# Block products for the gates of four more tiles in the first pass of a float32 macaron layer, later weight loads, and two reordered steps of the attention and drain stages

## The chip, the cores and the metric

The kernel runs on one core of one Trainium2 chip. The metric is device microseconds (us) of one execution. A core has five engines with a queue of instructions each: TensorE (PE in the profile; its weight loads are PEld), VectorE (DVE), ScalarE (ACT), GpSimd (POOL) and SyncE (SP, which here only issues DMAs). Each queue runs in order, and an instruction may wait for semaphores that other engines or DMAs raise.

## What is computed

The reference, cut to what matters (x is 4 x 1024 x 1024 in float32, so 4096 tokens of 1024 channels; the FFN weight is 1024 x 1024; there are 64 centroids):

```python
def _L0_ffn_ref(input, weight, bias, centroids, assignments):
    dots = softmax(x @ centroids.T / 0.1)          # gates: one row of 64 for each token
    hits = dots > 0.01
    query_sel = any(hits, axis=1)                  # which tokens are kept
    row_sel = any(hits, axis=0)[assignments]       # which output columns are kept
    dense = x @ weight.T + bias
    return where(query_sel[:, None] & row_sel[None, :], dense, 0)

x = x + 0.5 * _L0_ffn_ref(_layernorm(x), ...)
x = x + _L0_attn_ref(_layernorm(x), ...)           # attention among the 32 heads of one token
x = x + 0.5 * _L0_ffn_ref(_layernorm(x), ...)
```

`row_sel` needs the gates of all tokens before any column can be kept or dropped. So each FFN is a pass over all tokens for its products and gates, and the masked addition comes in the pass behind it.

## The kernel before

The 4096 tokens are 32 tiles of 128. There are three passes over them: the first FFN's products and gates (lines 511 to 791), the attention with the first FFN's masked addition ahead of it and the second FFN's gates behind it (lines 794 to 1174), and the second FFN's products and final addition (lines 1177 to 1263). Weights stay in SBUF: `wc` holds the 1024 columns of the FFN weight (transposed) with the 64 centroid columns behind them, `wqkv` holds the 768 columns of query, key and value (the four query heads of a group summed to one).

**Products of two tiles at once.** `winograd` (L293) computes columns 0 to 767 of two tiles a and b (a pair) with seven half products in place of eight: sums of the two tiles' activations (`token_sums`, L271, four POOL subtractions or additions: s1 to s4, of 128x512 each, in two "row" tiles named ts) meet sums of weight blocks (`weight_sums`, L262: ts, in the tiles ws). It is a generator with a `yield` behind each product, so that the loop around it sets where each product stands. Its order is product 1 (into a PSUM bank u), 5 (into v), 2, then 6 added onto u, 7 (into y), 3, then 4 added onto y. DVE adds each bank to the result row at L306; product 6 can only start once DVE has read u, and 4 once it has read y. `last_two` (L372) does the same for the 320 columns behind column 767, of which the last 64 are the gates: seven products of 160 columns each (L389, tiles la) with weight sums of their own (`te`, two of which lie in buffers that are used for something else later: `mask` and `bqkv`). Where a tile does not use it, `ffn_part` (L244) computes the 320 columns with eight plain products (L241, tiles ff).

**First pass.** Tiles 0 to 3 and 28 to 31 get their gates from `logits` (L684: ff products, then `gate` at L430 on DVE: maximum and subtraction). For tiles in `GATED`, here 8 to 27, `last_two` runs in step with `winograd` (L730 to 733). Tiles 4 to 7 are not in it and use `logits` too. The loop over t (L708) issues for each t, in this order: loads of later tiles on SP, stores of finished pairs on SP, normalization of tile t+1 on ACT (L535), moments of tile t+4 on DVE (L170), `logits` of tile t if it is not in GATED, the first product of the current pair, the block transpose of tile t+1 on DVE (L235), the scales of tile t+4, the exponentials of gates on ACT (L443), the other products (four in all at odd t, three at even t), `gated` (L446, four DVE operations for each tile that end with an update of `best`, L455), one step of `esums` (the sums te, one POOL subtraction each) at t = 5 to 8, token sums at odd t, and last a step of `weights(t)` (L601): one load of Wq (SP, 512 KB) with a reduction on DVE one iteration later (L612) at t = 3 to 5 and 11 to 15, and loads of Wk and Wv with copies on POOL (L627) at t = 16 to 19. The pair a = t - 3 and a + 1 is in work at odd t and at t + 1.

**Attention pass.** The loop over s (L1018) works on the projections of tile s, the attention of tile b = s - 2, the output of tile g = s - 3 and the gates of tile f = s - 4 or a = s - 5. From s = 4 projections are done by pairs (`project_two`, L813, the same seven products; its product 5 needs s1 of the pair's token sums, tiles ts_2q). At odd s the POOL queue holds, in order: `keys` (L888), `second_added` (L975, L979: the attention's result onto x), a store of x (L1051), `store_2` of two tiles (L996, L997: four DMA issues), `first_added` of tile s + 3 (L504: the first FFN's masked rows onto x; the mask itself is applied on DVE at L493), and then the four token sums of the pair that starts at s + 1 (L1095). At the next s, ACT reads that tile s + 3 at L196.

**Drain of the attention pass.** From s = 32 no new tile starts, and pairs of the second FFN's products (`winograd` on banks of the shared pool, weight sums in `wqkv`) fill PE. `gates_used` (L1007) runs `gated` for each tile whose gates are done. At s = 34 (NT + 2) it stands at the head of the step (L1052), ahead of three products of the pair 28, 29 (L1102); behind them on DVE come the moments of tile 31 (L170), then the adds of u and v (L306) behind product 6. On PE, product 6 is followed by the transpose of tile 30 (L218) and the ff products of tile 29 (L241), whose PSUM bank is the one that v had.

Of the kernel before, what the change touches and what calls it, by code (L numbers as in the profile page):

```python
# [32 lines left out]
PARTS = ((0, HALF), (HALF, 2 * HALF), (2 * HALF, EMB + NCL))  # L33
KEPT = 6
LAST = 2 * HALF, (EMB + NCL) // 2 - HALF
GATED = range(8, 28)
PAIRED = range(4, 32)
WARM = 16
ROWS = 26
# [3 lines left out]
def kernel(  # L43
# [42 lines left out]
    NT = xf.shape[0] // P  # L86
# [60 lines left out]
    def row(name):  # L147
        return data.tile([P, EMB], F32, tag="row", bufs=ROWS, name=name)
# [62 lines left out]
    def transposed(xn, name):  # L211

        t_ = row(f"xT_{name}").rearrange("p (k c) -> p k c", c=P)
        for h in range(2):
            tp = bank(f"tp_{name}_{h}").rearrange("p (j c) -> p j c", j=4)
            for j in range(4):
                k = 4 * h + j
                nc.tensor.transpose(tp[:, j, :], channels(xn)[:, k], ident)  # L218
            nc.scalar.copy(t_[:, 4 * h : 4 * h + 4, :], tp)  # L219
        return t_  # L220
# [225 lines left out]
    def gated(es, t, which):  # L446

        e, sm = es
        nc.vector.reciprocal(sm, sm)
        top = small.tile([P, 1], F32, tag="gtop", name=f"gtop_{which}_{t}")  # L450
        nc.vector.tensor_reduce(top, e, AX.X, ALU.max)
        nc.vector.tensor_scalar(
            qsel[which][:, t : t + 1], top, sm, THRESHOLD, ALU.mult, ALU.is_gt
        )
        nc.vector.scalar_tensor_tensor(best[which], e, sm, best[which], ALU.mult, ALU.max)  # L455
# [55 lines left out]
    with (  # L511
# [89 lines left out]
        def weights(t):  # L601


            if 3 <= t < 6 or 11 <= t < 16:

                k = t - 3 if t < 6 else t - 8
                qn = row(f"qn{k}").rearrange("p (c r) -> p c r", r=REP)
                nc.sync.dma_start(
                    out=qn.rearrange("p c r -> p (c r)"), in_=channel_rows(wq)[k]
                )  # L610
                yield
                nc.vector.tensor_reduce(  # L612
                    by_head(wqkv[:, k, :], 0),
                    qn.rearrange("p (d g) r -> p d g r", g=HKV),
                    AX.X,
                    ALU.add,
                )
            elif 16 <= t < 20:
                k = 2 * (t - 16)
                kvs = row(f"kv{k}").rearrange("p (k w c) -> p k w c", k=2, w=2)  # L620
                for i, src in ((0, wk), (1, wv)):
                    for j in range(2):
                        nc.sync.dma_start(out=kvs[:, j, i], in_=channel_rows(src)[k + j])
                yield
                for j in range(2):
                    for i in range(2):
                        nc.gpsimd.tensor_copy(  # L627
                            by_head(wqkv[:, k + j, :], i + 1),
                            kvs[:, j, i].rearrange("p (d h) -> p d h", h=HKV),
                        )  # L630
            elif 20 <= t < 24:

                nc.sync.dma_start(out=wtd[t - 20], in_=blocks(wc)[t - 20])
            elif t == 25:
                next(qsums)
            elif t == NT - 4:
                asg = load_assigned()
                yield
                hot.append(one_hot(asg))
            elif t == NT - 3:  # L640
                bn = row("bn_q").rearrange("p (c r) -> p c r", r=REP)
                nc.sync.dma_start(
                    out=bn.rearrange("p c r -> p (c r)"),
                    in_=bq.rearrange("d h -> (d h)").partition_broadcast(P),
                )
                bss = row("bs")
                bs = {i: bss[:, (i - 1) * D * HKV : i * D * HKV] for i in (1, 2)}
                for i, src in ((1, bk), (2, bv)):
                    nc.sync.dma_start(
                        out=bs[i], in_=src.rearrange("d h -> (d h)").partition_broadcast(P)  # L650
                    )
                yield
                nc.vector.tensor_reduce(
                    by_head(bqkv, 0), bn.rearrange("p (d g) r -> p d g r", g=HKV), AX.X, ALU.add
                )
                for i in bs:
                    nc.gpsimd.tensor_copy(
                        by_head(bqkv, i), bs[i].rearrange("p (d h) -> p d h", h=HKV)
                    )

        pending = iter(())
        sc, sb, ss, es, ge = {}, {}, {}, {}, {}
# [45 lines left out]
        for t in range(3, NT):  # L708

            loads(t)  # L710
            for i in (5, 6) if t == 3 else (t + 3,):
                if i in sc:
                    sb[i] = spread(sc.pop(i), i)
            if t % 2 == 1 and t > 4:
                for i in (a, a + 1):
                    nc.sync.dma_start(out=d1[i], in_=dt_.pop(i))
            ahead_b = t + 1 in sb and t > 3
            if ahead_b:
                blocks_normed(t + 1, sb.pop(t + 1))
            if t + 4 < NT:  # L720
                mv = moments(xt.pop(t + 4), f"1_{t + 4}")
            if t not in GATED:
                es[t] = logits(t)
            if t == 3:
                xT[4] = transposed(xn.pop(4), "1_4")
            if t % 2 == 1:
                a = t - 3
                s4 = ss.pop(a)
                steps = winograd(a, a + 1, s4, ts, psum1, 1, held=t == NT - 1)
                if a in GATED:  # L730
                    for i in (a, a + 1):
                        dt_[i] = row(f"d1_{i}")
                    steps = zip(steps, last_two(a, a + 1, s4, te, ge))
            if t < NT - 1:
                next(steps)
            if ahead_b:
                xT[t + 1] = from_blocks(t + 1, 1)
            if t + 4 < NT:
                block_scales(t + 4, mv)
            for i in sorted(es):  # L740
                if i >= t - 3 and not isinstance(es[i], tuple):
                    es[i] = gate_exp(es[i], i, 0)
            if t == NT - 1:
                for i in sorted(es):
                    gated(es.pop(i), i, 0)
                break
            for _ in range(2 + t % 2):
                next(steps)
            for i in (t - 3, t) if t < 6 else sorted(es):
                gated(es.pop(i), i, 0)  # L750
            if t % 2 == 0:
                for i in sorted(ge):
                    es[i] = gate_exp(ge.pop(i), i, 0)
            if 5 <= t < 9:
                next(esums)
            if t % 2 == 1:
                ss[t - 1] = token_sums(xT, t - 1, t, 1)
            for _ in pending:
                pass
            pending = weights(t)  # L760
            next(pending, None)

        xn2, xT2 = {}, {}
# [28 lines left out]
    with (  # L794
# [190 lines left out]
        es = {}  # L985

        def has(t):
            return 0 <= t < NT
# [18 lines left out]
        def gates_used():  # L1007
            for a in sorted(es):
                gated(es.pop(a), a, 1)
                if a < FIRST_KEPT:  # L1010
                    store_2(a)
# [6 lines left out]
        for s in range(NT + 5):  # L1018
            b, g, f, a = s - 2, s - 3, s - 4, s - 5
            paired, odd = s in PAIRED, s % 2 == 1  # L1020
# [28 lines left out]
                next(sums)  # L1049
            if g >= 0 and g < FIRST_KEPT:  # L1050
                nc.gpsimd.dma_start(out=y2[g], in_=xt[g])  # L1051
            if (odd or not paired) and s not in (NT, NT + 1):  # L1052
                gates_used()
            if s == 4:
                next(qsums)
# [30 lines left out]
            if paired and odd:  # L1086
                gate_2(a)
                qkv[s] = rearranged(flat.pop(s), s)
                fo = attend(st, qkv.pop(b)[1], b)
                if s + 2 in xn2:  # L1090
                    xT2[s + 2] = transposed(xn2.pop(s + 2), f"2_{s + 2}")
                if s + 3 in dt_ and has(s + 3):
                    first_added(s + 3)
                if s + 1 in PAIRED:
                    ss2 = token_sums(xT2, s + 1, s + 2, "2q")  # L1095
            if paired and not odd:
                fo = attend(st, qkv.pop(b)[1], b)
                if has(s + 2):
# [1 line left out]
            if s == NT + 2:  # L1100
                dt_[a] = row(f"d3_{a}")
                steps = winograd(s - 6, s - 5, ss, ts, None, 3)  # L1102
                for _ in range(3):
                    next(steps)
            for _ in range({NT: 3, NT + 1: 2}.get(s, 0)):
                next(steps)
            if NT <= s < NT + 2:
# [19 lines left out]
            else:  # L1127
                between()
                k = s - NT
# [15 lines left out]
            if odd and not paired and s + 1 in PAIRED:  # L1145
                xT2[s + 2] = transposed(xn2.pop(s + 2), f"2_{s + 2}")
                ss2 = token_sums(xT2, s + 1, s + 2, "2q")
            if 1 <= s <= 3:
# [3 lines left out]
                i = {1: NT - 4, 3: NT - 2}.get(s)  # L1152
# [24 lines left out]
    with (  # L1177
# [30 lines left out]
        t = NT - 2  # L1208
# [98 lines left out]
```

## Time and profile before

| | us |
|---|---|
| three runs | 1303.0 median (1300.79 to 1303.44) |
| profiled execution | 1301.45 |
| its span, first to last instruction | 1299.7 |
| mean granted TensorE clock in it | 0.998 |
| first pass, PE's first ff to the end of the pairs before 404 us | 14 to 404 |
| attention pass with its start and drain | 404 to 1040 |
| third pass | 1040 to 1300 |
| busy: PE, PEld, DVE, ACT, POOL | 1286.0, 833.2, 889.2, 490.4, 641.1 |

All rows below come from the profiled execution. Times in them count from the start of its span; a line such as L306 is a line of the kernel before. In a row of the timeline, the columns are start, duration, engine, line, operation, names of output and inputs, shape, count, and in brackets the engine's idle time ahead of it and what ended it. One matmul of the program shows as two records in float32, so eight plain products of a tile are 16 records, and one half product (four matmuls) is eight. Records of PE overlap, because matmuls are pipelined: what a group costs PE is the time from its start to the start of the next, not its duration.

### The profile page before, as it was taken

The page shows a single profiled execution, that of the slowest core. Times are in us where ns is not written, and L with a number is a line of the kernel's source. Part 1 is how long each engine was busy: PE and PEld are TensorE (multiplying, and loading weights), DVE is VectorE, ACT ScalarE, POOL GpSimd, SP SyncE. Part 2 cuts the span into 40 slices and gives each one's busy share as a digit, 9 for nine tenths or more (in the row PEclk, how much of TensorE's full clock was granted, in tenths as well). Part 3 has the DMA queues.
Part 4 walks back from the last instruction along what each step waited for, and adds up shares of the span by engine and source line. Part 5 has one row for each costly group of instructions (what it writes and reads, how often), then busy time and mean ns, then how long its engine had stood idle before and what let it go on. Part 6 is the DMA issues. An engine that isn't in the chain of part 4 may idle for free.

```text
span 1299.7 us, 22528 instructions
## 1 busy us (share of the span) xinstructions
PE 1286.0 (99%) x8634; PEld 833.2 (64%) x8634; DVE 889.2 (68%) x1810; ACT 490.4 (38%) x792; POOL 641.1 (49%) x512
## 2 busy tenths in 40 slices
PE   8999999999999999999999999999999999999998
PEld 7665677777776666666666666666666655555555
DVE  4566667665646358888888888888877449555556
ACT  4443332333210446666676676666633300000000
POOL 2631212312113256777877777776857417533440
PEclk9999999999999999999999999999999999999999
DMA  8645645654114156577777777777552347665522
GB/s 302 143 150 150 177 158 150 182 195 137 60 57 194 44 168 199 175 219 222 226 216 232 236 223 223 225 235 214 173 161 61 106 158 222 235 211 181 175 111 85
DMA packets 191124, 227.08 MB, mean 175 GB/s; under 512 B 118184, under 2 KB 146728, under 8 KB 191016
## 3 DMA queue, kind: packets, MB, share of 16 engines
q1 hardware_dynamic: 170892, 171.33, 44.4%
q0 software_dynamic: 11232, 37.49, 8.3%
q10 hardware_dynamic: 8892, 16.81, 3.6%
q8 instruction: 68, 1.11, 0.4%
q14 instruction: 40, 0.33, 0.1%
HBM read 134.59 MB, written 90.99 MB: 174 GB/s over the span
## 4 chain that ended last, share of the span: by engine, by line
PE 87%; DVE 5%; POOL 3%; ACT 2%; DMA 2%; issue 2%; SPq 0%; ACTq 0%; POOLq 0%
PE st L315 43%; PE qs L832 16%; PE ff L241 11%; PE la L389 6%; PE pq L241 3%; PE tp L218 3%; PE po L950 2%; PE sc L908 2%; DVE o L962 1%; DVE bn L170 1%; DMA qk<-qkvd 1%; PE tpw L584 1%; POOL wqkv L268 1%; DMA cn<-in_L_ffn_centroids_dram 0%; DVE d L493 0%
## 5 line engine op out<-in xcount | busy, mean ns | idle before, releaser
L280 POOL TENSOR_TENSOR ts<-xT 128x512 f32<-128x512 f32 x32 | 41.9, 1309 | 358.9 <-DVE sc L179 159.0
L241 PE MATMUL ff<-wc,xT 128*128 128x320 f32 x704 | 197.1, 433 | 1.3 <-ACT xT L219 0.6
L306 DVE TENSOR_TENSOR d<-st,d 128x384 f32<-128x384 f32 (+1 forms) x162 | 88.7, 549 | 155.7 <-PE st L315 154.5
L315 PE MATMUL st<-wc,xT 128*128 128x384 f32 x512 | 175.8, 486 | 0.0
L241 PEld LDWEIGHTS ff<-wc,xT 128*128 128x128 f32 x704 | 131.9, 190 | 56.2 <-ACT xT L219 1.5
L315 PEld LDWEIGHTS st<-wc,xT 128*128 128x128 f32 x512 | 95.9, 190 | 61.8 <-issue 0.6
L315 PE MATMUL st<-wqkv,ts 128*128 128x384 f32 (+1 forms) x392 | 129.7, 480 | 2.1 <-DVE d L306 1.9
L315 PE MATMUL st<-ws,ts 128*128 128x384 f32 x384 | 131.1, 486 | 0.0
L832 PE MATMUL qs<-wc,ts_2q 128*128 128x384 f32 x336 | 114.6, 491 | 1.8 <-POOL ts_2q L280 1.8
L315 PEld LDWEIGHTS st<-wqkv,ts 128*128 128x128 f32 x392 | 73.8, 190 | 52.9 <-POOL x L979 2.4
L306 DVE TENSOR_TENSOR d<-st,brow 128x384 f32<-128x384 f32 x96 | 52.8, 550 | 74.4 <-PE st L315 74.3
L888 POOL TENSOR_TENSOR kd<-qk,tmask 128x1024 f32<-128x1024 f32 x32 | 62.6, 1955 | 82.6 <-DMA qk<-qkvd 82.4
L173 ACT ACTIVATE mv<-mv,eps 128x1 f32<-128x1 f32 x66 | 19.5, 295 | 216.8 <-DVE mv L172 216.5
L504 POOL TENSOR_TENSOR x<-x,d 128x1024 f32<-128x1024 f32 x32 | 75.7, 2366 | 48.3 <-DVE d L493 44.6
L315 PEld LDWEIGHTS st<-ws,ts 128*128 128x128 f32 x384 | 71.2, 190 | 43.0 <-issue 0.8
L832 PEld LDWEIGHTS qs<-wc,ts_2q 128*128 128x128 f32 x336 | 62.5, 190 | 46.0 <-POOL ts_2q L280 3.0
L493 DVE SCALAR_TENSOR_TENSOR d<-d,qsel,mask 128x1024 f32<-128x1024 f32 (+2 forms) x68 | 88.4, 1299 | 0.2
L315 PE MATMUL st<-wc,ts 128*128 128x384 f32 x256 | 87.9, 486 | 0.0
L170 DVE BATCH_NORM_STATS2 bn<-x 128x6 f32<-128x512 f32 x132 | 84.2, 679 | 3.0 <-DMA x<-in_L_attn_x_dram 3.0
L979 POOL TENSOR_TENSOR x<-x,ot 128x1024 f32<-128x1024 f32 x32 | 80.3, 2509 | 2.5
L219 ACT COPY xT<-tp 128x512 f32<-128x512 f32 x112 | 59.5, 582 | 52.6 <-PE tp L218 52.6
L832 PE MATMUL qs<-wqkv,xT 128*128 128x384 f32 x224 | 78.3, 492 | 0.0
(147 smaller groups left out, 2309.3 us busy)
## 6 DMA issues: line engine op xcount, KB each, us to landing
x<-in_L_attn_x_dram SPq DMA_DIRECT2D x64, 512.0 KB
d<-d SPq DMA_DIRECT2D x64, 512.0 KB
out_dram<-x ACTq DMA_DIRECT2D x30, 512.0 KB
xb<-in_L_attn_x_dram SPq DMA_DIRECT2D x108, 128.0 KB
y<-x POOLq DMA_DIRECT2D x26, 512.0 KB, 4.1
xTd<-xT POOLq DMA_DIRECT2D x26, 512.0 KB, 6.1
xT<-xTd SPq DMA_DIRECT2D x26, 512.0 KB
x<-y SPq DMA_DIRECT2D x26, 512.0 KB
```

What stands on the lines that cost most here:

```text
L170: nc.vector.bn_stats(st[:, i, :], src[:, i * 512 : (i + 1) * 512])
L219: nc.scalar.copy(t_[:, 4 * h : 4 * h + 4, :], tp)
L241: nc.tensor.matmul(p, src[:, k, :], wts[:, k, lo:hi], start=(k == 0), stop=(k == KT - 1))
L280: nc.gpsimd.tensor_tensor(s1, a21, a22, ALU.add)
L306: nc.vector.tensor_tensor(out, ps, other, ALU.add)
L315: nc.tensor.matmul(ps, src[:, k, :], wts[:, k, :], start=(k == 0 and onto is None), stop=(k == 3), skip_group_check=onto is not None,)
L389: nc.tensor.matmul(ps, src[:, k, :], wts[:, k, :], start=(k == 0 and onto is None), stop=(k == 3), skip_group_check=onto is not None,)
L493: nc.vector.scalar_tensor_tensor(d[:, sl], d[:, sl], qsel[which][:, t : t + 1], mask[:, sl], ALU.mult, ALU.mult)
L504: nc.gpsimd.tensor_tensor(xt[t], xt[t], dt_.pop(t), ALU.add)
L832: nc.tensor.matmul(ps, src[:, k, :], wts[:, k, :], start=(k == 0 and onto is None), stop=(k == 3), skip_group_check=onto is not None,)
L888: nc.gpsimd.tensor_tensor(kd, qk[:, :, D:].unsqueeze(2).to_broadcast([P, NBLK, 4, D]), tmask.unsqueeze(1).unsqueeze(3).to_broadcast([P, NB ...
L979: nc.gpsimd.tensor_tensor(xv, xv, ov, ALU.add)
```

## The change

It has three parts. In the first pass, `GATED` begins at tile 4: the pairs 4, 5 and 6, 7 run `last_two`, and the `logits` of those four tiles go. For that, the four `esums` steps stand at t = 3 to 6, the eight loads of Wq with their reductions at t = 7 to 14 and the loads of Wk and Wv at t = 15 to 18. In the attention pass at odd s, s1 and s2 of the token sums stand ahead of `first_added` on POOL, and s3 and s4 behind it. In the drain at s = 34, `gates_used` stands behind the three products of the pair 28, 29 in place of ahead of them.

```diff
-GATED = range(8, 28)
+GATED = range(4, 28)
...
         def weights(t):
-            if 3 <= t < 6 or 11 <= t < 16:
-                k = t - 3 if t < 6 else t - 8
+            if 7 <= t < 15:
+                k = t - 7
...
-            elif 16 <= t < 20:
-                k = 2 * (t - 16)
+            elif 15 <= t < 19:
+                k = 2 * (t - 15)
...
             for i in (t - 3, t) if t < 6 else sorted(es):
-                gated(es.pop(i), i, 0)
+                if i in es:
+                    gated(es.pop(i), i, 0)
...
-            if 5 <= t < 9:
+            if 3 <= t < 7:
                 next(esums)
...
-            if (odd or not paired) and s not in (NT, NT + 1):
+            if (odd or not paired) and not NT <= s <= NT + 2:
                 gates_used()
...
+                more = []
+                if s + 1 in PAIRED:
+                    ss2 = token_sums(xT2, s + 1, s + 2, "2q", more)
                 if s + 3 in dt_ and has(s + 3):
                     first_added(s + 3)
-                if s + 1 in PAIRED:
-                    ss2 = token_sums(xT2, s + 1, s + 2, "2q")
+                for i in more:
+                    i()
...
                 steps = winograd(s - 6, s - 5, ss, ts, None, 3)
                 for _ in range(3):
                     next(steps)
+                gates_used()
```

With a list as its last argument, `token_sums` issues s1 and s2 and appends a function that issues s3 and s4.

## Prediction

> **What bounds the kernel now.** I read the page first, then PE's waits, then the timelines of the three places that the change touches.
>
> ```profile
> span 1299.7 us, 22528 instructions
> PE 1286.0 (99%) x8634; PEld 833.2 (64%) x8634; DVE 889.2 (68%) x1810; ACT 490.4 (38%) x792; POOL 641.1 (49%) x512
> PE st L315 <- DVE d L306: 1.9, 1, 1.9
> PE qs L832 <- POOL ts_2q L280: 1.8, 2, 1.4
> PE ff L241 <- DVE d L306: 0.4, 1, 0.4
> ```
>
> The first two lines are of the page, the others of PE's waits (who, for whom, us in total, times, longest). PE is at work for 99% of the span, so time goes only where PE issues less or waits less. Every other engine has a third of the span free: what the change moves there is free until it makes PE wait. Three of the listed waits lie where the change works, 4.1 us together; the rest (tile loads at the start and the like) it does not touch.
>
> A busy PE need not be at its pace, so I took the distances from start to start. In the first pass they repeat to the nanosecond:
>
> ```profile
> 90.81 4.47 PE L241 MATMUL ff<-wc,xT 128*128 128x320 f32 x16
> 95.11 2.74 PE L315 MATMUL st<-wc,xT 128*128 128x384 f32 x8
> ...
> 133.81 1.25 PE L389 MATMUL la<-wc,xT 128*128 128x160 f32 x8
> 134.90 2.74 PE L315 MATMUL st<-ws,ts 128*128 128x384 f32 x8
> 137.48 1.25 PE L389 MATMUL la<-te,ts 128*128 128x160 f32 x8
> ```
>
> A plain gate product costs 95.11 - 90.81 = 4.30 (4.31 at the others), a narrow block product 134.90 - 133.81 = 1.09, a wide one 137.48 - 134.90 = 2.58.
>
> **Part 1, gates of tiles 4 to 7.** Removed: four ff products, 4 x 4.31 = 17.2. Added: two pairs of seven la products, 14 x 1.09 = 15.2. PE gains 2.0. A check by stages: pair 2, 3 with its two ff takes 68.60 to 95.28, 26.68; pair 8, 9 takes 131.23 to 156.90, 25.67; the difference is 1.01 for each pair.
>
> The narrow products are not new to the trace: it has 70 of them, all at this pace, against the same weights. A row that could speak against them is PEld's 190 ns for each load: 112 loads in a row would be 21.3, 4.1 more than the ff products took. But eight la records start within 1.09, 136 ns each, so most of each load is under the matmul before it. The Trainium skill, "TensorE: Matmul & The Clock Gate", section "LDWEIGHTS (loading the stationary operand)", gives a load by its columns over 1.2, which would be an estimate of 107 ns here, below 136; by that page too nothing is added. I take 0.
>
> What moves. PE reaches pair 4, 5 earlier by three ff products (those of tiles 4, 5 and 6), at about 82 in place of 95. What must be there by then:
> - te: POOL needs 1.55 for each. One comes ahead of the sums of pair 2, 3 (43.6 to 45.2), two behind them (50.2 to 53.3), the last behind the sums of pair 4, 5 (about 66). Their first uses are from 82 on. The sums of pair 2, 3 end 1.6 later, at 50.2, and PE needs them at 62.6.
> - Tiles 5 to 7 are not needed by PE at their own t any more, but with their pairs. DVE transposed tile 5 at 59.65 to 61.67, tile 7 at 86.3 to 88.3; with PE ahead these come earlier still, for their inputs (ACT at 48.75 for tile 5) were there.
> - SP loses three loads of 512 KB in its busiest stretch (46.9, 53.1, 67.8) and gets them at t = 7 to 10 instead, where one for each t stands beside the same stores and loads as at t = 11 to 15 now; PE has no wait there. DVE's reductions (1.2 each) go with them.
> - PE passes tiles 4 to 6 at 7.7, 10.3, 7.7 each. It does so now at t = 8 to 10 (105 to 131) without a wait.
>
> One place is tight, at t = 4. DVE does the gates of tiles 0 and 3 (53.82 to 55.08) and the moments of tile 8 (to 56.6) ahead of the add of product 7, which would end at 57.15. Product 4 writes the same bank and can start at 52.25 + 2 x 2.58 = 57.41. Margin 0.26. The `best` operations in that stretch took 0.28 each while POOL was idle; where POOL ran, at 65.24 and 66.10, they took 0.50 and 0.87. Stretched like the longer, two would add 1.2 and PE would wait 0.9. POOL now works there until 53.3, while the first `best` comes at 54.25: clear by 0.95. Bounds 0 to 0.9; I take 0. The Trainium skill, "SBUF — State Buffer", section "Who interferes with whom", makes this an exclusive lock between DVE and GpSimd for an instruction with two SBUF inputs, so that a `best` which meets POOL waits it out, up to 1.55; by that rule the cost is all or nothing, and the 0.95 decides it.
>
> **Part 2, token sums ahead of the addition.** Product 5 of a pair waits for s1, which stands on POOL behind `first_added`:
>
> ```profile
> 908.12 2.36 POOL L504 TENSOR_TENSOR x<-x,d 128x1024 f32<-128x1024 f32 x1
> 910.43 1.26 POOL L280 TENSOR_TENSOR ts_2q<-xT 128x512 f32<-128x512 f32 x1
> 911.75 2.52 PE L832 MATMUL qs<-wc,ts_2q 128*128 128x384 f32 x7 [1.36 <-POOL ts_2q L280]
> ```
>
> Without L504 ahead of it s1 ends 2.3 earlier. Its input, the transposed tile, left ACT at 902.97, so nothing else holds it. The waits of 1.36 and of 0.40 (at 602.82) go: 1.7 by start to start. In the other pairs s1 ended 0.5 to 1.4 ahead of product 5 (636.12 against 637.07), so nothing is gained there; a margin of about 3 replaces it. s3 and s4 end as before.
>
> The price is that x of tile s + 3 is ready 2.5 later, when s2 ended until now. Its reader is ACT's L196 at the next s. In an ordinary pair: x would end at 637.5, L196 starts at 639.12, margin 1.6. In the pair above: 913.0 against 912.29, so ACT is late by 0.7; DVE asks for the outcome at 918.47 (L202), and ACT's last step for it ended at 916.3. Hidden. Bounds: 0 to a delay on twelve steps (rival 4). I take 0. `keys`, which stands behind s4, keeps its time.
>
> **Part 3, gates of tile 28 behind three products.**
>
> ```profile
> 1012.37 0.16 DVE L449 RECIPROCAL gsm<-gsm 128x1 f32<-128x1 f32 x1 [3.03 <-ACT ge L443]
> ...
> 1012.81 1.46 DVE L455 SCALAR_TENSOR_TENSOR best<-ge,gsm,best 128x64 f32<-128x64 f32 x1
> 1014.20 0.54 DVE L306 TENSOR_TENSOR d<-st,brow 128x384 f32<-128x384 f32 x1
> 1014.84 0.56 DVE L306 TENSOR_TENSOR d<-st,d 128x384 f32<-128x384 f32 x1
> ...
> 1014.88 2.82 PE L315 MATMUL st<-wqkv,ts 128*128 128x384 f32 x8 [1.86 <-DVE d L306]
> ...
> 1018.94 1.34 PE L241 MATMUL ff<-wc,xT 128*128 128x320 f32 x4 [0.35 <-DVE d L306]
> ```
>
> DVE stood for 3 us on ACT's exponential with the add of u queued behind it, and product 6 waited for that add. With the add first it runs at 1009.4, and product 6 starts at 1010.28 + 2.58 = 1012.86, 2.0 earlier. But that is not all gain, for the next wait takes over. After product 6 (to 1015.45) and the transpose (0.98, to 1016.4) comes ff of tile 29, which needs v's bank, and v's add stands behind the moments of tile 31. DVE then: second add 1013.05, `gated` from 1013.55, its `best` at 1014.0 and over by 1014.3 (now it lasts until POOL's addition of x for tile 31 ends at 1014.19). Moments at 1014.3 in place of 1015.32, which is also the floor that this x sets. They and ACT's root take 2.3 (1015.32 to 1017.61), so the adds start at 1016.6, v's starts 0.6 later and takes 0.56: ff at 1017.8 in place of 1018.94. Gain 1.1. Bounds: 0, since the same DVE work lies ahead of the moments as before and cannot end later, to 2.2 if v's bank came free at once. I take 1.1. From there on PE runs without waits to its end, so the gain stays.
>
> **The sum.** 2.0 + 1.7 + 1.1 = 4.8 against the profiled execution: 1301.45 - 4.8 = 1296.65, span 1294.9 (1.75 lie around it). The runs' median is 1303.0, 1.55 above that execution. If those runs had more of the second wait, part 2 removes it as well and they end at 1296.65 too; if it is something else, 1298.2. The second wait hangs on chance delays of POOL's chain, such as its 2.43 of "issue" ahead of a DMA at 903.5, so I lean to the first: **1297.0**.
>
> **Rivals.** (1) The drain comes out at a bound: nothing gained there, 1297.0 + 1.1 = 1298.1; for it, two waits in a row on one DVE queue; or the full 2.2, 1295.9. (2) Part 2 gains nothing, because something else is late for product 5: 1298.7, or up to 1300.2 from the median. Against it, s1's inputs were there 5 us or more before. (3) A new wait of 2 to 4 in the quicker tiles 4 to 8 eats part 1: 1299 to 1301. For it, the margin of 0.26; against it, that it costs at most 0.9 there, and margins of 10 elsewhere. (4) Slower: x of tile s + 3 comes too late in all twelve reordered steps, and ACT's delay goes on to DVE's L202 and to the adds that free PE's banks. ACT's margin is 1.6 and DVE's another 1.5 (609.0 against 610.5), so POOL would have to run over 3 us later than traced, each time; for the gain of 4.8 to become a loss of 2.6 takes 7.4 / 12 = 0.6 beyond it: 1305.6 and more. That the change is not done is no case: in the built order ff of tiles 4 to 7 is gone, la stands in its place, and POOL and DVE stand as described.
>
> **Chances.** Forecast 0.60 (1295 to 1298); (1) 0.10 at either end; (2) 0.08; (3) 0.08; (4) 0.04. A difference under 0.2% (2.6 us) is about what these runs cannot tell from no change. Faster, below 1300.4: 0.60 + 0.20 + 0.08 = 0.88; the same: (3), 0.08; slower: 0.04. From 1294.8, where the full drain gain meets the fastest run, to 1300.0 lie over 8 in 10.
>
> **What would show it.** The page: ff x640, la x672, PE busy 2.0 less between 52 and 131 (pair 8, 9 starting 2.0 earlier). PE's waits: "qs <- POOL ts_2q" gone, "st <- DVE d L306" gone, "ff <- DVE d L306" grown from 0.4 to about 1.4. Wrong would be: a wait of st or la in 52 to 131, a wait of qs for DVE that was not there, or a third pass that does not simply shift.

## The result, and the profile after

The changed kernel takes 1297.99 us (median of 17 runs, 1295.26 to 1302.55), against 1303.0 (1300.66 to 1307.68, 17 runs) for the kernel before in the same comparison: a ratio of 0.9959, 95% interval 0.9948 to 0.9969, so 5.0 us or 0.4% faster. The forecast was 1297.0, with a range of 1294.8 to 1300.0.

The profiled execution of the changed kernel, at 1300.42 us, lies near the slow end of its runs. These are lines of its page (span and busy times; the group of the ff products, whose last columns are the idle time ahead of it and what ended it):

```profile
span 1298.7 us, 22641 instructions
...
PE 1284.8 (99%) x8682; PEld 836.7 (64%) x8682; DVE 897.9 (69%) x1826; ACT 485.2 (37%) x788; POOL 637.6 (49%) x512
...
L241 PE MATMUL ff<-wc,xT 128*128 128x320 f32 x640 | 179.3, 433 | 2.2 <-DVE d L306 1.2
```

PE's waits in it (us in total, times, longest), which answer to those shown of before:

```profile
PE qs L833 <- DVE sc L202: 2.7, 5, 0.9
...
PE qs L833 <- DVE qkv L866: 1.3, 5, 0.5
PE ff L241 <- DVE d L306: 1.2, 1, 1.2
```

(Lines of the attention pass are one higher than before: L833 was L832, L980 was L979.) "qs <- POOL ts_2q" and "st <- DVE d L306" are gone, and the drain's ff wait grew from 0.4 to 1.2, as forecast. But qs now waits 4.0 us for DVE, in two lines. Of before, PE's waits show only the second of them, with one wait:

```profile
PE qs L832 <- DVE qkv L865: 0.2, 1, 0.2
```

The prediction had named just such a wait as a sign that it was wrong.

It helps to cut the span where PE's own instructions mark it, and to do so for every profiled kernel. The columns are: PE's start at t = 3, a matter of the first loads; from there to the product bT that closes the first pass; from bT to the drain's first st of the pair 28, 29; from that st to the ff of tile 29; from that ff to the end; and the number, of 13, of L493 at even s that took over 1.7 us in place of 1.2. The first row is the kernel before, and the sum of the five times is the span.

| kernel | to t = 3 | part 1: to bT | to the drain | part 3: st to ff | rest | long L493 |
|---|---|---|---|---|---|---|
| before | 41.76 | 366.48 | 596.88 | 13.82 | 280.76 | 2 |
| part 1 alone | 42.52 | 364.46 | 599.03 | 13.85 | 280.75 | 6 |
| part 2 alone | 40.20 | 366.48 | 600.87 | 13.84 | 280.75 | 5 |
| part 3 alone | 41.67 | 366.48 | 599.20 | 12.54 | 280.75 | 5 |
| parts 1 and 3 | 41.34 | 364.46 | 600.56 | 12.53 | 280.77 | 7 |
| changed kernel | 41.12 | 364.47 | 599.83 | 12.54 | 280.75 | 7 |
| changed, second profile | 40.82 | 364.46 | 596.05 | 12.54 | 280.78 | 3 |

Parts 1 and 3 stand out to a few hundredths in every kernel that has them: 2.02 and 1.28. The stretch between them, the second pass, spreads over 3.7 us in the four kernels without part 2 and over 4.8 us in the three executions with it; two executions of the changed kernel differ by 3.8. So one profile of each kernel could not say what part 2 does, and the new waits had to be traced first. One of the five places, in the timeline of the changed kernel:

```profile
810.93 2.35 POOL L980 TENSOR_TENSOR x<-x,ot 128x1024 f32<-128x1024 f32 x1
811.37 2.99 DVE L493 SCALAR_TENSOR_TENSOR d<-d,qsel,mask 128x1024 f32<-128x1024 f32 x1
812.06 0.29 ACT L199 ACTIVATE sd<-sd,eps 128x1 f32<-128x1 f32 x1
...
814.28 0.55 DVE L854 TENSOR_TENSOR qkv<-qs,bqkv 128x384 f32<-128x384 f32 x1
814.86 0.56 DVE L855 TENSOR_TENSOR qkv<-qs,qkv 128x384 f32<-128x384 f32 x1
815.34 0.15 DVE L202 RECIPROCAL sc<-sd 128x1 f32<-128x1 f32 x1
```

L493, the masked multiplication of `first_added` at even s, begins 0.44 behind POOL's addition L980 and ends 1.08 after it (813.28 to 814.36). It ends 1.08 or 1.09 after L980 at 570.40, 775.93 and 846.86 too, so it stands still until POOL is done, and the profile books the standstill as DVE's busy time. The adds L854 and L855, which free PE's banks, queue behind it; product 3 then starts at 815.57 with a wait of 0.88. The wait is put down to L202, the neighbour of the add. (The expectations below call this product 2; it is product 3, the one with wqkv and ts_2q.) ScalarE's sd was there at 812.35, 3.0 ahead of L202, so x was not late (rival 4).

### The profile page after: what moved, and what is told of

Read it like the earlier page. It is cut to its first block, busy times and chain, and to the rows that moved or that the text cites. A ratio compares the mean times of both kernels' runs of the same rounds, so it can differ in the third digit from the quotient of the medians.

```text
span 1298.7 us, 22641 instructions
## 1 busy us (share of the span) xinstructions
PE 1284.8 (99%) x8682; PEld 836.7 (64%) x8682; DVE 897.9 (69%) x1826; ACT 485.2 (37%) x788; POOL 637.6 (49%) x512
## 4 chain that ended last, share of the span: by engine, by line
PE 84%; DVE 7%; ACT 4%; DMA 2%; POOL 2%; issue 1%; SPq 0%; ACTq 0%; DVEq 0%; POOLq 0%
PE st L315 43%; PE qs L833 13%; PE ff L241 10%; PE la L389 7%; PE pq L241 3%; PE tp L218 3%; PE po L951 2%; PE sc L909 2%; DVE d L493 1%; DVE o L963 1%; DVE bn L170 1%; POOL wqkv L268 1%; ACT xn L188 1%; ACT xT L219 1%; PE tpw L584 1%
## 5 line engine op out<-in xcount | busy, mean ns | idle before, releaser
L306 DVE TENSOR_TENSOR d<-st,d 128x384 f32<-128x384 f32 (+1 forms) x162 | 88.6, 549 | 153.2 <-PE st L315 152.1
L241 PE MATMUL ff<-wc,xT 128*128 128x320 f32 x640 | 179.3, 433 | 2.2 <-DVE d L306 1.2
L241 PEld LDWEIGHTS ff<-wc,xT 128*128 128x128 f32 x640 | 119.8, 190 | 51.5 <-DVE d L306 1.4
L833 PE MATMUL qs<-wc,ts_2q 128*128 128x384 f32 x336 | 114.4, 490 | 0.0
L306 DVE TENSOR_TENSOR d<-st,brow 128x384 f32<-128x384 f32 x96 | 52.8, 550 | 72.2 <-PE st L315 72.2
L504 POOL TENSOR_TENSOR x<-x,d 128x1024 f32<-128x1024 f32 x32 | 75.5, 2359 | 47.9 <-DVE d L493 45.3
L493 DVE SCALAR_TENSOR_TENSOR d<-d,qsel,mask 128x1024 f32<-128x1024 f32 (+2 forms) x68 | 97.2, 1430 | 0.2
L833 PEld LDWEIGHTS qs<-wc,ts_2q 128*128 128x128 f32 x336 | 62.6, 190 | 43.7 <-issue 3.2
L980 POOL TENSOR_TENSOR x<-x,ot 128x1024 f32<-128x1024 f32 x32 | 79.0, 2470 | 2.5
L833 PE MATMUL qs<-wqkv,xT 128*128 128x384 f32 x224 | 78.3, 492 | 0.0
```

The source lines that it names most:

```text
L241: nc.tensor.matmul(p, src[:, k, :], wts[:, k, lo:hi], start=(k == 0), stop=(k == KT - 1))
L306: nc.vector.tensor_tensor(out, ps, other, ALU.add)
L493: nc.vector.scalar_tensor_tensor(d[:, sl], d[:, sl], qsel[which][:, t : t + 1], mask[:, sl], ALU.mult, ALU.mult)
L504: nc.gpsimd.tensor_tensor(xt[t], xt[t], dt_.pop(t), ALU.add)
L833: nc.tensor.matmul(ps, src[:, k, :], wts[:, k, :], start=(k == 0 and onto is None), stop=(k == 3), skip_group_check=onto is not None,)
L980: nc.gpsimd.tensor_tensor(xv, xv, ov, ALU.add)
```

## The experiments

The first theory on this trace: part 2 makes POOL reach L980 earlier, so that L493 more often comes second; part 2 then gives back what it gains. The rival was x of tile s + 3 arriving late. Each kernel was timed against the kernel before, and its ratio is to that.

**The three parts by themselves.** Each is the kernel before with the hunks of one part (one line of each shown):

```diff
# part 1 alone
-GATED = range(8, 28)
+GATED = range(4, 28)
# part 2 alone
+                    ss2 = token_sums(xT2, s + 1, s + 2, "2q", more)
# part 3 alone
+                gates_used()
```

> The kernel before with part 1 alone (gates of tiles 4 to 7 in block products, weights behind tile 6, sums of the centroids at t = 3 to 6). Theory: TensorE issues 2.0 us less and nothing waits for it, so 2.0 us faster than before (about 0.9985). Pair 8, 9 starts 2.0 earlier by the trace, the attention pass is as before apart from chance. Rival (the loads or the gates make a wait in tiles 4 to 8): a wait of st or la between 52 and 131 and a gain under 1.

> The kernel before with part 2 alone (first two sums of tokens ahead of the addition at odd s). As predicted: the waits of qs for POOL ts_2q go, 1.7 us faster, nothing else. Theory formed on the trace of after: the waits go, but POOL's x addition of even s (L980 in after) now begins ahead of DVE's masked multiplication (L493) in more pairs; where it begins first, L493 takes 2.5 to 3.0 in place of 1.2, TensorE's product 2 waits 0.4 to 1.0 for the adds behind it, and the gain is between 0 and 1.7, with some 3 to 6 such pairs. Rival (x of tile s + 3 late at ACT): ACT's L196 starts late in the pairs that wait and DVE's L202 waits for sd.

> The kernel before with part 3 alone (gates of tile 28 behind three products of the drain). Theory: 1.1 to 1.3 us faster, the stretch from the st product at 1005 to the ff of tile 29 at about 12.5 in place of 13.8, and everything ahead of it as before. Rival: the drain's gain is lost again before the end, under 0.5.

Measured: part 1 1301.22 us, 0.9973 (0.9962 to 0.9984); part 2 1301.97, 0.9978 (0.9965 to 0.9992); part 3 1302.51, 0.9988 (0.9977 to 0.9999). Each gains, part 3 barely outside the noise. The wait that the theory gave to part 2 is there without it; PE's waits of part 1 alone:

```profile
PE qs L833 <- DVE sc L202: 2.2, 3, 1.2
PE qs L833 <- DVE qkv L866: 1.1, 4, 0.5
```

That was the first blow to the theory: this kernel has the second pass of before, and six long L493 against seven in the changed one.

**The changed kernel again, and without part 2.** The second is the changed kernel with this taken back:

```diff
-                    ss2 = token_sums(xT2, s + 1, s + 2, "2q", more)
                 if s + 3 in dt_ and has(s + 3):
                     first_added(s + 3)
-                for i in more:
-                    i()
+                    ss2 = token_sums(xT2, s + 1, s + 2, "2q")
```

> The changed kernel once more, as the neighbour of the three below, and for a second profile. Theory (pairs in which POOL's addition begins ahead of DVE's masked multiplication come by chance): the pairs with a long L493 are others than in the first profile, between 2 and 8 of 13 at even s; time 0.995 to 0.997 of before. Rival (the five pairs are set by the order of the program): the same five pairs, 573, 779, 814, 850 and 885.

> Parts 1 and 3 without part 2. As predicted: 1.7 slower than the changed kernel, with one or two waits of qs for POOL ts_2q, 1 to 3 us together. Rival (part 2 gives back in collisions of L493 what it takes from these waits): within 0.7 of the changed kernel, and fewer long L493.

Measured, on one chip: 1297.71 us, 0.9946 (0.9933 to 0.9958), and 1300.66, 0.9974 (0.9962 to 0.9985). The second profile of the changed kernel has three long L493 where the first had seven. Those three pairs (at 500, 570 and 912) had a long one in the first profile too, and the one at 500 has it in all seven rows of the table, without a wait of PE: that one does not come by chance. Gone are the four between 776 and 882. In the pair in which DVE was held at 846.86 in the first profile, the order was now the other way round (its timeline):

```profile
844.15 1.19 DVE L493 SCALAR_TENSOR_TENSOR d<-d,qsel,mask 128x1024 f32<-128x1024 f32 x1
844.18 1.75 POOL L976 TENSOR_TENSOR ot<-ot,rs 128x256 f32<-128x256 f32 x1 [0.43 <-DMA ot<-od]
846.01 2.37 POOL L980 TENSOR_TENSOR x<-x,ot 128x1024 f32<-128x1024 f32 x1
```

Here DVE was first by 0.03, and POOL's L976 took 1.75 in place of its 0.73; PE did not wait. L976 was late because `keys` ahead of it ended only 0.39 before L493 began (1.62 in the first profile), and because its load came in 0.43 after POOL was free. So which of the two is held is set by when that load and POOL's chain land, pair by pair. Without part 2 (before, part 1, part 3, parts 1 and 3) there were 2, 6, 5 and 7 long ones, with it 5, 7 and 3: the same mean of 5. The theory that part 2 causes them falls. Without part 2 the time is 3.6 us longer in this comparison (0.9974 less 0.9946, intervals apart) and 2.0 against the first one (0.9959, intervals overlapping), so its gain is kept.

**Is it a lock between DVE and POOL?** The changed kernel without the multiplication by the column mask at L493:

```diff
-        masked(dt_[t], t, 0, mask)
+        nc.vector.tensor_scalar(dt_[t], dt_[t], qsel[0][:, t : t + 1], None, ALU.mult)
```

> The changed kernel with the multiplication by the column mask left out of first_added in the second pass: DVE's operation there is then a tensor_scalar with one SBUF operand of full size and a scalar for each row. Theory (DVE's and POOL's two-operand instructions shut each other out): that operation is never longer than its normal time even where POOL's addition runs beside it, POOL's additions at even s are never 3.2, and the waits of qs for DVE at product 2 and at L866 are gone, 3 to 5 us faster than the changed kernel's own neighbour. Rival (the operation is slowed by whatever else uses SBUF, or DVE is late for another reason): it is long in some pairs as before and the waits stay.

Measured 1296.29 us, 0.9937 (0.9923 to 0.9952). In its profile PE never waits for a bank or a sum in the pairs: bT to the drain takes 594.21, the shortest of all, 1.8 to 6.7 us less than in the seven rows above. But its median is only 1.4 to 1.7 us below those of the changed kernel, not 3 to 5 (its interval overlaps that of its neighbour, 0.9933 to 0.9958), and the operation with one full-size operand was held as well (its timeline):

```profile
500.15 2.36 POOL L980 TENSOR_TENSOR x<-x,ot 128x1024 f32<-128x1024 f32 x1
501.72 1.33 DVE L503 TENSOR_SCALAR d<-d,qsel 128x1024 f32<-128x1024 f32 x1
```

It takes 0.65 to 0.75 when undisturbed, 1.33 here and 2.10 at worst. So "two operands" was too narrow. The Trainium skill, "SBUF — State Buffer", section "Who interferes with whom", has DVE and GpSimd share one pair of ports under an exclusive lock, for a DVE instruction with two SBUF inputs (against a GpSimd one that reads SBUF) and for a tensor_scalar in a two-port mode; whoever issues first keeps it for the whole instruction. Both forms and both orders show in these rows (2.99, 1.75, 1.33). That the tensor_scalar ran in such a mode no row says; that it was held one does. Some rows with L493 at odd s do not go by the order of the recorded starts; they come with the last kernel below.

**Moving L493 out of the way on DVE.** Three kernels keep the operation and move it or POOL's addition. First, the bank adds ahead of L493 at even s:

```diff
-                if has(s + 3):
-                    first_added(s + 3)
                 next(two)
+                if has(s + 3):
+                    first_added(s + 3)
```

> The changed kernel, and at even s product 6 with its two adds is issued ahead of first_added(s + 3), so that DVE's two bank adds no longer stand behind the masked multiplication L493. Theory (POOL's x addition holds L493, and only the adds behind it make TensorE wait): the waits of qs for DVE at product 2 and the later ones at L866 go, some 4.5 us in the profiled execution; 2 to 4 us faster than the changed kernel's 1298.0, so 1294 to 1296, with L493 still long in the same pairs or shorter. Rival (x of tile s + 3 late): x comes another 1.1 later for every tile, so no gain, or 1 to 5 slower.

Second, both masks of a pair at odd s, ahead of the sums over po (shown in part; `first_added` then leaves the mask of these tiles out):

```diff
                 qkv[s] = rearranged(flat.pop(s), s)
+                for i in (s + 3, s + 4):
+                    if i in dt_ and has(i):
+                        masked(dt_[i], i, 0, mask)
                 fo = attend(st, qkv.pop(b)[1], b)
```

> The changed kernel, and at odd s the masked multiplications of tiles s + 3 and s + 4 are both issued ahead of the sums over po (L961, L963), in the 2.8 us in which POOL only issues transfers, so that none stands at even s. Theory: no collision at even s, DVE's adds there come 1.2 us or more earlier, the waits of qs for DVE at product 2 and L866 go, and no new wait comes at odd s (sc there has 2.8 of margin, of which 2.5 is used): 2 to 4 faster than the changed kernel, about 1294 to 1296 against 1298. Rival: the two operations meet POOL at odd s, or delay po's bank, and sc waits up to 1 us in 14 pairs: 2 to 10 slower.

Third, L980 behind `first_added` on POOL at even s (shown in part; `second_added` returns its addition instead of issuing it):

```diff
                 if has(s + 3):
                     first_added(s + 3)
+                x_added()
                 next(two)
```

> The changed kernel, and at even s POOL adds the attention's output to x (L980) behind the addition of first_added and not ahead of it, so that POOL stands waiting for L493 while L493 runs. Theory: L493 at even s is never long except behind the scaling of ot (0.7) or keys, the waits of qs for DVE at product 2 go as with the split multiplication; but DVE's moments of that tile wait up to 1 us for the later x, and product 4 waits for the add behind them: between 2 faster and 2 slower than the changed kernel. Rival (the waits come from x being late, not from the lock): no change in the waits at product 2.

All three are slower than the changed kernel, though the first two were expected 2 to 4 faster: 1304.30 us (0.9997, 0.9987 to 1.0007), 1305.05 (1.0007, 0.9996 to 1.0018) and 1305.65 (1.0015, 1.0002 to 1.0028). The adds ahead of L493 make it start about 1.1 later, so mostly behind L980; 9 of the 13 are long. In its timeline the adds are in time, and what follows L493 is late instead, down to the bank of po:

```profile
818.45 2.35 POOL L980 TENSOR_TENSOR x<-x,ot 128x1024 f32<-128x1024 f32 x1
...
819.32 0.56 DVE L855 TENSOR_TENSOR qkv<-qs,qkv 128x384 f32<-128x384 f32 x1
819.80 2.08 DVE L493 SCALAR_TENSOR_TENSOR d<-d,qsel,mask 128x1024 f32<-128x1024 f32 x1
821.81 0.15 DVE L202 RECIPROCAL sc<-sd 128x1 f32<-128x1 f32 x1
```

Its waits of PE:

```profile
PE sc L909 <- DVE o L963: 3.6, 5, 1.4
PE qs L833 <- DVE qkv L866: 3.5, 8, 0.6
```

The two masks at odd s cost u's add (L849, here L852) its time. The margin that I had counted was that of sc; what ran short was this add further down DVE's queue, as the waits of PE show:

```profile
PE qs L836 <- DVE qkv L852: 6.0, 11, 0.7
```

With L980 behind L504, only one L493 at even s is long, and the wait at product 3 is gone, which bears out that L980 was what held it. But DVE's moments now wait for x, and product 4 for the add behind them. From its timeline and its waits of PE:

```profile
821.75 1.29 DVE L170 BATCH_NORM_STATS2 bn<-x 128x6 f32<-128x512 f32 x2 [0.53 <-POOL x L980]
```

```profile
PE qs L833 <- DVE qkv L866: 4.5, 11, 0.7
```

The price was put at up to 2 and is over 7. In all three, PE waits about 0.5 for DVE in most pairs: at none of the three places that were tried had DVE's queue the time to give.

**Taking the work off DVE.** POOL multiplies by the column mask, and DVE only by the row selection; then the same with the drain reordered; then, with both, ScalarE in DVE's place (shown in part):

```diff
     def first_added(t, split=False):
+        if split:                                   # at even s
+            nc.vector.tensor_scalar(dt_[t], dt_[t], qsel[0][:, t : t + 1], None, ALU.mult)
+            nc.gpsimd.tensor_tensor(dt_[t], dt_[t], mask, ALU.mult)
# drain reordered, s = 34
+                if k == 2:
+                    next(steps)
                 between()
# with ScalarE
-            nc.vector.tensor_scalar(dt_[t], dt_[t], qsel[0][:, t : t + 1], None, ALU.mult)
+            nc.scalar.activation(dt_[t], dt_[t], AF.Identity, scale=qsel[0][:, t : t + 1])
```

> The changed kernel, and at even s the masked multiplication is split: DVE multiplies by the selection of the rows (0.65 to 0.75 us by the run without the mask), POOL by the mask of the columns (about 2.35), ahead of its addition. Theory (a long L493 ahead of the bank adds is the only thing that makes TensorE wait in the second pass, and POOL has 4 us free behind the addition at even s): the waits of qs for DVE go; 1 to 2.5 faster than the changed kernel (median 1297.7 to 1298.0), about 1295.5 to 1297, and a narrower spread of its runs. Rival (the longer POOL chain delays x of tile s + 3, the loads of blocks that POOL issues, or the sums of the next pair): waits of qs for POOL ts_2q or of L235 come, same or slower.

> The kernel with the split multiplication, and in the drain product 6 and its three adds are issued ahead of the normalization of tile 31 (moments, adds, then reciprocal and scaling in place of moments, reciprocal, scaling, adds). Theory: ff of tile 29 starts about 0.7 to 0.9 earlier (its wait for d L306 falls from 1.2 to 0.4), and the scaling of tile 31, which ends 1.6 later, is not needed by TensorE until 1030: 0.8 faster than the kernel with the split alone, which the trace shows and the times may not. Rival: the transpose of tile 31 or the gates behind it wait.

> As the split multiplication with the reordered drain, but ScalarE and not DVE multiplies by the selection of the rows at even s (an Identity with a scale for each row, 1.0 to 1.25 us by its neighbours L196 and L208), so that DVE has nothing there that POOL could hold. Theory (a DVE operation that POOL shuts out is the whole of the remaining waits in the second pass): no wait of qs for DVE at even s, the stretch from bT to the drain's first st takes 594.2 to 594.6 as in the kernel without the mask, and the time is 1294 to 1295.5, 2.5 to 4 faster than the changed kernel. ScalarE has 3.0 us free between L199 and L208 there. Rival (ScalarE's scaling stands ahead of L208 or of an exponential): a wait of tp or xb's reader for xn, or of qs, in each of 13 pairs, and no gain against 1297.

Measured: 1297.61 us (0.9948, 0.9935 to 0.9962), 1297.02 (0.9943, 0.9926 to 0.9960) and 1295.64 (0.9927, 0.9907 to 0.9946). The split alone changes nothing that the times show: DVE's shorter operation is still held now and then, and waits of qs for DVE stay, 0.6 and 0.8 us in total. The drain's reordering does what was expected, 12.54 to 11.73 from st to ff, with PE's wait there down to

```profile
PE ff L241 <- DVE d L306: 0.3, 1, 0.3
```

In that profile the stretch from ff to the end was 282.20 and not 280.8, all of it behind PE's last product; in the kernel with ScalarE, with the same drain, it was 280.77 again.

ScalarE does it without being held, although POOL runs L984 (the former L980) beside it. Its timeline:

```profile
845.98 0.56 DVE L859 TENSOR_TENSOR qkv<-qs,qkv 128x384 f32<-128x384 f32 x1
846.00 1.14 ACT L504 ACTIVATE d<-d,qsel 128x1024 f32<-128x1024 f32 x1
846.22 2.37 POOL L984 TENSOR_TENSOR x<-x,ot 128x1024 f32<-128x1024 f32 x1
847.04 2.17 ACT L208 ACTIVATE xn<-x,sc 128x1024 f32<-128x1024 f32 x1
...
849.49 2.37 POOL L505 TENSOR_TENSOR d<-d,mask 128x1024 f32<-128x1024 f32 x1
851.93 2.37 POOL L508 TENSOR_TENSOR x<-x,d 128x1024 f32<-128x1024 f32 x1
```

L504 takes 1.13 to 1.14 in all 13 pairs. No bank add waits at even s; bT to the drain takes 595.36, a little over the 594.2 to 594.6 expected, with one wait of 0.8 left at an odd s, where L493 met a token sum:

```profile
797.79 3.21 DVE L493 SCALAR_TENSOR_TENSOR d<-d,qsel,mask 128x1024 f32<-128x1024 f32 x1
...
798.63 1.27 POOL L280 TENSOR_TENSOR ts_2q<-xT 128x512 f32<-128x512 f32 x1
```

Here L493 began 0.84 ahead of the sum by the record and was held all the same, to 1.09 after its end. Three more rows at odd s are like this one, with leads of 0.91 (part 2 alone, 661.45), 0.29 (L980 behind L504, 524.82) and 0.26 (without the mask, 525.00). So the earlier recorded start does not always win; why is open.

This is the fastest kernel of the study: beyond doubt faster than the kernel before, and 2.1 and 2.4 us below the changed kernel's medians, 0.8 of it from the drain. Its interval lies below the first of the changed kernel's two and overlaps the second (0.9933 to 0.9958), so that lead is likely and not settled.

## Why the prediction was right, and where it was off

- **Part 1, −2.0.** Right to 0.02: 366.48 to 364.46 in every kernel with it. No wait of st or la came (rival 3). The tight place, with a margin of 0.26 at t = 4, held with 0.23: the add of product 7 ends at 56.38 and product 4 starts at 56.61. (The 57.41 took 52.25 from the chain; from start to start it is 52.09 + 5.16 = 57.25, which makes the forecast margin 0.10.) The two `best` ahead of it took 0.28 and 0.27, so neither met POOL. A weight load of la shows as 190 ns in both kernels, not as the estimated 107; the 0 for it held all the same. By the times alone part 1 is worth 3.5 (2.1 to 5.0); the trace shows 2.0 in the stretch that it changes, and what else the times hold is not explained.
- **Part 2, −1.7.** The step was right: no profile of a kernel with it shows "qs <- POOL ts_2q", while the kernel before, part 3 alone and parts 1 and 3 show 1.8, 2.9 and 0.5 us of it. Part 1 alone shows 0.1, so this wait comes by chance too, and 1.7 was the value of one execution; the mean of the four is 1.3. The times give 2.9 (1.0 to 4.6) for it alone, and 2.0 or 3.6 beside the others. Its size is not settled more closely, and the profiles do not show the gain in the second pass: its mean is 598.9 in the four kernels without part 2 and 598.9 in the three executions with it. That x comes later cost nothing at ScalarE in the pair traced above. (The L202 that the prediction has at 918.47 starts at 918.29; nothing hangs on it.)
- **Part 3, −1.1.** 13.82 to 12.54, so 1.28. The mechanism was as forecast: one wait goes, and the ff of tile 29 waits for v's bank behind the moments of tile 31. In the changed kernel:

```profile
1013.16 2.74 PE L315 MATMUL st<-wqkv,ts 128*128 128x384 f32 x8
...
1014.27 0.32 DVE L455 SCALAR_TENSOR_TENSOR best<-ge,gsm,best 128x64 f32<-128x64 f32 x1
1014.54 1.29 DVE L170 BATCH_NORM_STATS2 bn<-x 128x6 f32<-128x512 f32 x2
...
1017.34 0.56 DVE L306 TENSOR_TENSOR d<-st,d 128x384 f32<-128x384 f32 x1
...
1017.96 4.58 PE L241 MATMUL ff<-wc,xT 128*128 128x320 f32 x16 [1.17 <-DVE d L306]
```

- **The lean to 1297.0.** Between 1296.65 and 1298.2 I leaned to the first, supposing that the 1.55 by which the runs of before exceed their profiled execution was more of the wait that part 2 removes. That was the step that was off. The second pass of that execution was short, 596.88 with two long L493, against 599.0 to 600.6 with five to seven in the other three kernels without part 2. The wait for POOL ts_2q is 1.2 on the mean in those three (0.1, 2.9 and 0.5), less than the 1.8 of that execution, while qs waits 3.3, 1.2 and 4.2 for DVE against 0.2. So, as far as four profiles tell, the excess is mostly these collisions, which the change does not touch, and the changed kernel came out at 1298.0, beside the 1298.2 of the other branch.
- **Luck.** That 4.8 lies so close to the measured 5.0 is in part luck: parts 1 and 3 are 3.3 together in every trace, but the wait that the third term counts on came out between 0.1 and 2.9 in four profiles.
- **The sign that I named.** "A wait of qs for DVE that was not there" came up and meant nothing about the change: it was already in the program, and the profiled execution of before showed 0.1 of it at 542 and 0.2 at 551. A single execution's list of waits is no test where a wait comes by chance.
- **Rival 4** (x too late, slower) had the right engine and the wrong cause: DVE's adds are late in places, but through POOL holding L493, not through x.

## What to carry to other kernels

Cut the span at marks on the engine that bounds it, and compare the stretches over several variants: here what the change did was constant to a few hundredths of a us, and what wandered was chance, however well it seemed to fit a story. When an operation on one engine is sometimes twice as long, see whether it ends a fixed time after an operation of another engine (here 1.08 after POOL's); if so, try the work on an engine whose time does not change beside that one. Here that helped (ScalarE), while moving it within the same full queue only moved the wait.

## What the runs showed of the hardware

- A DVE instruction that POOL holds shows as busy, not idle: at even s L493 took 1.19 alone and up to 3.32 in the rows of the table, ending 1.08 or 1.09 after POOL's. With DVE first by 0.03 us the loss was POOL's (1.75 in place of 0.73). The recorded starts do not always tell which is held: in four rows at odd s DVE began 0.26 to 0.91 ahead and was held.
- A one-operand multiplication of 128x1024 on DVE, 0.65 alone, is held too (1.33, 2.10), while ScalarE's took 1.13 to 1.14 in all 13 pairs, 11 of them beside a POOL operation on SBUF tiles.
- Two executions of the changed kernel differ by 3.8 us in the second pass (596.05 and 599.83), with 1.1 and 4.0 us of such waits of qs for DVE. In the first profile four pairs in which DVE was held follow one another (776 to 882). That one such pair sets up the next, because PE slips by 1 us and POOL does not, fits this but was not tried.
